# Preparing a scan layer's first chunk between the matmuls of the convolution before it

## The chip, the cores and the metric

The kernel runs on one core of one Trainium2 chip. All of it is float32. The metric is the device time of one execution in microseconds (us); of several runs the median is taken. The profile is of one execution. Engines are called PE (TensorE), DVE (VectorE), ACT (ScalarE), POOL (GpSimd) and SP (SyncE, which issues most of the DMAs); SBUF is the on-chip memory and PSUM the eight banks that matmuls write.

## The reference

Four residual layers on an image batch `x` of shape (3, 256, 48, 48). `_gn` is a group norm.

```python
x = x + _L0_conv_ref(_gn(x), ...)   # convolutions and attention blocks
x = x + _L1_conv_ref(_gn(x), L1_conv_routing_ws, L1_conv_weight)  # 3x3, weights mixed per image from 8 experts
x = x + _L2_conv_ref(_gn(x), L2_conv_weight, L2_conv_bias)        # 3x3
x = x + _L3_conv_ref(_gn(x), ...)   # selective scan (Mamba)
```

The change touches the border between the third and the fourth. The fourth takes the 2304 pixels of an image as a sequence `xf`:

```python
xn = (xf - mu) * jax.lax.rsqrt(var + 1e-05) * norm_w + norm_b     # over the 256 channels
x_in, z = jnp.split(jnp.einsum('blc,dc->bld', xn, in_proj_w), 2, axis=-1)
u = jax.nn.silu(depthwise causal conv of x_in over 4 positions + conv_b)
x_dbl = jnp.einsum('bld,ed->ble', u, x_proj_w)                    # dt_raw, B_ssm, C_ssm
dt = jax.nn.softplus(jnp.einsum('blr,dr->bld', dt_raw, dt_proj_w) + dt_proj_b)
# step: h = h * exp(dt_t * A) + dt_t * B_t * u_t;  y_t = h . C_t
y = (y + u * D_param) * jax.nn.silu(z)
out = jnp.einsum('bld,cd->blc', y, out_proj_w)
```

## The kernel before

**Layers 1 and 2** are one loop (L970 to L1002) over six units, layer by image, images in the order 2, 1, 0. Each unit has two halves `h`, each half two channel blocks `m`. An `output` (L943) makes six `products`: each is six matmul calls over 288 columns into one PSUM bank of the pool `ps` (seven banks, tag `c`). A call becomes two PE instructions. Products come as two pairs, each pair read by ACT (`cb`, L952) and DVE (`add`, `sub`, L954 and L956), then eight DVE updates of the image in SBUF (L961 to L964), then two single products, each read by one DVE update (L966). Beside them DVE transforms the next half's input (`input_transform`) and, in units 0 to 2, mixes the next unit's weights `u` (L271, L273). At the end of an image of layer 2 its six chunks are stored to DRAM (`xd`, L994) and its group norm is taken (matmuls L182 and L191, result in `norm3`).

**Layer 3** works in 18 chunks of 384 positions (six per image) and, per chunk, eight steps of eight scans (`scan`, L1378), so 144 steps. Before the scans a chunk is prepared by stages that the table `plan` lists, one after the other by their data: `fetch` (from `xd`), `group_scale` (ACT), `less_mean` (PE), `centre` (ACT), `square_mean` (PE), `inverse_root` (ACT), `normalise` (DVE), `tokens` (ACT), `taps` of four blocks (PE, with the weights `wtap`) and `take_u` (ACT), `silu` (ACT), `project_u` (PE), `take_dbc` (ACT, then DMAs to DRAM and back, spread over partitions: `bcd`, `bc`), and twice `project_dt` (PE), `softplus` (ACT), `take_dt` (DVE), `keep_dt` (ACT, then two DMAs `dtd`, `dtud`). All matmuls of these stages write the two banks of `psg`. `spread` (L1310) then brings rows of `dtd` and `dtud` back by eight DMAs, `fill` writes the scans' input (half on DVE, L1341, half on POOL, L1345), `decay` (ACT, L1370) the scans' factors, `times_c` (POOL, L1386) and `add_states` (PE, L1403) collect the result.

In the steady state the stages of the next two chunks are dealt out over the steps of the current one (`run`). For chunk 0 they stand in front of the first step, one after the other, and so do the first seven of chunk 1. Ahead of them come the layer's own weights: four DMAs for `cwb`, one each for `w3sb`, `dtsb` and `winx`, and four DVE products that make `wtap` (L1031).

**Memory.** The pools of layers 1 and 2 (weights `up0` and `up1`, images `x0` to `x2`, `vp`, `pad`, `wst`) are closed before layer 3 opens its own over the same addresses; a tile there waits until the old tile's last reader is done.

**Order.** In the scan (and in the attention of layer 0) `keep_order` ties the instructions of PE, DVE, ACT and POOL to the order in which the program writes them. Elsewhere, and for SP always, the framework puts each engine's instructions in order when the kernel is built: earlier in the program first, but past one that it reckons not ready. On the chip each engine then follows its list.

Of the kernel before, what the change touches and what calls it, by code (L numbers as in the profile page):

```python
# [16 lines left out]
P = 128  # L17
# [66 lines left out]
def net(  # L84
# [27 lines left out]
    late_pools = ExitStack()  # L112

    def late_pool(name, bufs=1):
        return late_pools.enter_context(tc.tile_pool(name=name, bufs=bufs, side="right"))
# [238 lines left out]
    with ExitStack() as l0:  # L354
# [482 lines left out]
        xs[2] = late_pool("x2").tile([P, CT, N], F32, name="x2")  # L837
        upools = {0: late_pool("up0")}
        for b in (1, 0):
            xs[b] = late_pool(f"x{b}").tile([P, CT, N], F32, name=f"x{b}")  # L840
# [51 lines left out]
        for n, b in enumerate(ORDER):  # L892
# [11 lines left out]
            for c in range(NCH):  # L904
                concatenated(b, c, *ahead.pop(0))
                z = n * NCH + c + 3
                if z < len(chunks):
                    ahead.append(parts(*chunks[z]))
                if c:
                    take_stats(b, c - 1, stats)  # L910
                if b == 0 and c == 3:
                    vp = late_pool("vp", 2)
                    pad = late_pool("pad")
                    first_v = input_transform(2, 0, *norms[2])
                aside(3)
# [10 lines left out]

    with ExitStack() as l1:
        upools[1] = l1.enter_context(tc.tile_pool(name="up1", bufs=1))
        tmp = l1.enter_context(tc.tile_pool(name="tmp", bufs=2))
        ps = l1.enter_context(tc.tile_pool(name="ps1", bufs=7, space=PSUM))  # L930
# [13 lines left out]
        def output(b, h, m, u, vt, bias):  # L944
# [4 lines left out]
            for i, j in ((1, 3), (4, 5)):  # L949
# [7 lines left out]
                sums += [add, sub]  # L957
            p, q, r, s = sums
# [6 lines left out]
            for i, k, f in ((0, 0, 1.5), (2, 3, 6.0)):  # L965
                stt(xj[:, k], products(u, vt, m, i), f, xj[:, k], ALU.mult, ALU.add)  # L966

# [12 lines left out]

        vt = first_v
        for n, (k, h) in enumerate(halves):
            layer, b = units[k]
            ahead = transformed(n + 1) if n + 1 < len(halves) else None
# [6 lines left out]
            if layer and h == 1:  # L991
# [10 lines left out]
                norm3[b] = keep[:, 0, :], keep[:, 1, :]  # L1002

    late_pools.close()
# [5 lines left out]
    with ExitStack() as l3:  # L1010
        wp = l3.enter_context(tc.tile_pool(name="w3", bufs=1))
        act = l3.enter_context(tc.tile_pool(name="act", bufs=2))
        psd = l3.enter_context(tc.tile_pool(name="psd", bufs=1, space=PSUM))
        psr = l3.enter_context(tc.tile_pool(name="psr", bufs=1, space=PSUM))
        psg = l3.enter_context(tc.tile_pool(name="psg", bufs=1, space=PSUM))
        psy = l3.enter_context(tc.tile_pool(name="psy", bufs=1, space=PSUM))

        w3sb = wp.tile([P, NW3], F32, name="w3sb")
        nc.sync.dma_start(w3sb, w3)
        dtsb = wp.tile([DTR + 1, DI * P], F32, name="dtsb")  # L1020
        nc.sync.dma_start(dtsb, dtw)

        wtap = wp.tile([P, DCONV, CT, DI * P], F32, name="wtap")
        with tc.tile_pool(name="w3in", bufs=1) as wi:
            winx = wi.tile([P, CT, DI * P], F32, name="winx")
            nc.sync.dma_start(winx, w3x.rearrange("(t p) n -> p t n", p=P))
            cwb = wi.tile([P, DCONV, DI * P], F32, name="cwb")
            for k in range(DCONV):
                nc.sync.dma_start(cwb[:, k, :], convw[k : k + 1, :].broadcast_to([P, DI * P]))
            for k in range(DCONV):  # L1030
                nc.vector.tensor_tensor(  # L1031
                    wtap[:, k, :, :], winx,
                    cwb[:, k, :].unsqueeze(1).broadcast_to([P, CT, DI * P]), ALU.mult,
                )

        scn = l3.enter_context(tc.tile_pool(name="scn", bufs=2))

        def w(name, at, n):
            a = W3_AT[name] + at
            return w3sb[:, a : a + n]  # L1040


        amat = wp.tile([P, DI * DS], F32, name="amat")
        nc.scalar.activation(amat, v("A_log", 0, DI * DS), AF.Exp)
        nc.vector.tensor_scalar(amat, amat, -1.0, None, ALU.mult)

        rep = wp.tile([P, 4, 32], F32, name="rep")
        for r in range(4):
            nc.vector.tensor_reduce(
                rep[:, r, :], ident.rearrange("p (q d) -> p d q", d=32), AX.X, ALU.add  # L1050
            )
        fold = rep[:, 0, :]

        less = wp.tile([P, 2, P], F32, name="less")
        nc.vector.tensor_tensor(less[:, 0, :], ident, mean2, ALU.subtract)
        nc.vector.tensor_scalar(less[:, 1, :], mean2, -1.0, None, ALU.mult)
        zero = wp.tile([P, 8], F32, name="zero")
        nc.vector.memset(zero, 0.0)
# [4 lines left out]

        todo = [(b, c) for b in ORDER for c in range(NCH)]

        def fetch(at):
            k = chunks[at] = Chunk()
            k.b, k.c = todo[at]
            k.before = chunks.get(at - 1)
            k.xp = act.tile([P, CT, CH], F32, name="xp", bufs=1)  # L1070
            nc.sync.dma_start(k.xp, xd[k.b][:, k.c])

        class Chunk:
            pass


        bank = [psg.tile([P, 512], F32, name=f"ps_g{j}")[:, :CH] for j in range(2)]

        def in_order(t):

            return t.rearrange("p (j n) -> p n j", j=4)

        def group_scale(k):
            sc, sh = norm3[k.b]
            k.xg = act.tile([P, CT, CH], F32, name="xg", bufs=1)
            for ct in range(CT):
                nc.scalar.activation(
                    k.xg[:, ct, :].rearrange("p (n j) -> p j n", j=4),  # L1090
                    k.xp[:, ct, :].rearrange("p (j n) -> p j n", j=4), AF.Identity,
                    bias=sh[:, ct : ct + 1], scale=sc[:, ct : ct + 1],
                )

        def less_mean(k):

            for to in range(CT):
                for ct in range(CT):
                    nc.tensor.matmul(  # L1099
                        bank[to], less[:, int(to != ct), :], k.xg[:, ct, :],  # L1100
                        start=ct == 0, stop=ct == CT - 1,
                    )

        def square_mean(k):
            for ct in range(CT):
                nc.tensor.matmul(
                    bank[1], mean2, k.sq[:, ct, :], start=ct == 0, stop=ct == CT - 1
                )

        def centre(k):  # L1110
            for ct in range(CT):
                nc.scalar.copy(k.xg[:, ct, :], bank[ct])
            k.sq = act.tile([P, CT, CH], F32, name="sq", bufs=1)
            nc.scalar.activation(k.sq, k.xg, AF.Square)

        def inverse_root(k):
            var = bank[1]
            nc.scalar.activation(var, var, AF.Ln, bias=epst)
            nc.scalar.activation(var, var, AF.Exp, scale=-0.5)

        def normalise(k):
            rs = bank[1].unsqueeze(1).broadcast_to([P, CT, CH])
            nc.vector.tensor_tensor(k.xg, k.xg, rs, ALU.mult)

        def tokens(k):

            xn = k.xn = act.tile([P, CT, CH + DCONV - 1], F32, name="xn")
            if k.c == 0:
                nc.gpsimd.memset(xn[:, :, : DCONV - 1], 0.0)
            else:  # L1130
                nc.scalar.copy(xn[:, :, : DCONV - 1], k.before.xn[:, :, CH:])
# [73 lines left out]
        def keep_dt(k, m0):  # L1205
            for j in range(2):
                nc.scalar.copy(k.dt[:, m0 + j, :], bank[j])  # L1207
            if m0 == 0:
                k.dtd, k.dtud = {}, {}
# [376 lines left out]
```

## Time and profile before

| | |
|---|---|
| median of 3 runs | 3690.63 us (3689.73 to 3693.51) |
| profiled execution | 3692.94 us, span 3691.2 us, granted PE clock 0.926 |
| PE busy | 3195.5 us, 87% of the span |
| DVE busy | 3058.3 us, 83% |
| ACT busy | 2265.2 us, 61% |
| POOL busy | 1440.4 us, 39% |

The span runs from the first to the last instruction, and times below count from its start; the execution's own time is 1.74 us more. The page cuts the span into 40 slices of 92 us and gives each engine's busy share in tenths. In other rows a name such as `ps_c<-vt,u` gives what is written and what is read, `x264` how many instructions are merged in the row, and a bracket the time that the engine stood idle before it and what it waited for. `PEclk` is the granted share of PE's clock. A row that begins with `SPq` is a DMA being issued, not its transfer.

### The profile page before, as it was taken

The numbers are of one execution on the slowest core, as the hardware profiler recorded it, in microseconds if no ns is written. First come the engines' busy times: TensorE is split into PE (matmuls) and PEld (weight loads), VectorE is DVE, ScalarE is ACT, GpSimd is POOL, SyncE is SP. The second block draws the span as 40 slices with busy tenths as digits, with TensorE's granted clock in tenths as the row PEclk, the third lists the DMA queues.
The fourth block names the chain that finished last, engine by engine and source line by source line (L and its number), as shares of the span: only waits on it lengthen the run. The fifth ranks groups of instructions, "written<-read, shape, count | busy, mean of one in ns | idle before, by whom it ended". The sixth has DMA issues, their size and how long they took to land. (4 is left out here: it accounts for less than half of the span.)

```text
span 3691.2 us, 45621 instructions
## 1 busy us (share of the span) xinstructions
PE 3195.5 (87%) x17154; PEld 1442.3 (39%) x17154; DVE 3058.3 (83%) x3398; ACT 2265.2 (61%) x3402; POOL 1440.4 (39%) x386
## 2 busy tenths in 40 slices
PE   6999999999999998777799857888878888888885
PEld 4323232342323224455577633333333333333331
DVE  3798999869889993589977429999999999999997
ACT  2688787758878773320011037777777777777774
POOL 0000000000000001110000009999999999999998
PEclk9999999999999999888899978999889999988887
DMA  4000000000000003645401234444444444444441
GB/s 176 4 1 1 1 2 1 1 39 1 2 1 2 1 1 112 211 149 197 165 13 26 67 85 95 99 106 112 108 110 109 105 105 99 106 115 106 112 106 35
DMA packets 167672, 266.50 MB, mean 72 GB/s; under 512 B 42689, under 2 KB 133633, under 8 KB 165266
## 3 DMA queue, kind: packets, MB, share of 16 engines
q1 hardware_dynamic: 155346, 245.80, 24.7%
q10 hardware_dynamic: 12096, 17.70, 1.5%
q8 instruction: 136, 2.23, 0.3%
q14 instruction: 94, 0.77, 0.1%
HBM read 216.31 MB, written 46.89 MB: 71 GB/s over the span
## 5 line engine op out<-in xcount | busy, mean ns | idle before, releaser
L597 ACT ACTIVATE pt<-ps_s 128x1024 f32<-128x1024 f32 x972 | 938.9, 1022 | 236.9 <-PE ps_s L593 219.1
L1378 DVE TENSOR_TENSOR_SCAN hs<-ps_da,hs 128x385 f32<-128x385 f32 x1152 | 1012.9, 940 | 60.2 <-ACT ps_da L1370 43.7
L673 DVE TENSOR_TENSOR part<-part,pt 128x2048 f32<-128x2048 f32 x396 | 906.5, 2289 | 79.4 <-ACT pt L597 54.8
L1386 POOL TENSOR_TENSOR hc<-hs,bc 128x3072 f32<-128x3072 f32 x144 | 888.2, 6169 | 85.8 <-PE ps_g L1186 28.6
L1370 ACT ACTIVATE ps_da<-dtr,amat 128x384 f32<-128x384 f32 x1152 | 657.8, 582 | 317.2 <-DVE hs L1378 289.2
L162 POOL TENSOR_TENSOR rstd<-ve,mhalf 128x2 f32<-128x2 f32 (+1 forms) x26 | 17.3, 668 | 1650.4 <-DVE ve L160 1650.4
L593 PE MATMUL ps_s<-q,kt 32*128 32x512 f32 (+1 forms) x4320 | 614.6, 592 | 2.3 <-DVE q L554 0.9
L1345 POOL TENSOR_TENSOR hs<-dtur,bc 128x1536 f32<-128x1536 f32 x144 | 496.4, 3447 | 95.9 <-DMA dtur<-dtud 85.2
L606 PE MATMUL acc<-pt,vt 128*32 128x512 f32 (+1 forms) x4320 | 521.3, 561 | 8.1 <-DVE o L653 7.9
L937 PE MATMUL ps_c<-vt,u 128*128 128x288 f32 x1728 | 429.4, 411 | 66.6 <-DVE u L259 39.4
L937 PEld LDWEIGHTS ps_c<-vt,u 128*128 128x128 f32 x1728 | 331.1, 192 | 159.3 <-issue 46.1
L1142 PE MATMUL ps_g<-xn,wtap 128*128 128x384 f32 x1152 | 387.1, 491 | 3.0 <-ACT xn L1133 3.0
L593 PEld LDWEIGHTS ps_s<-q,kt 32*128 32x128 f32 x4320 | 220.1, 183 | 387.6 <-issue 225.4
L1142 PEld LDWEIGHTS ps_g<-xn,wtap 128*128 128x128 f32 x1152 | 214.3, 189 | 174.7 <-issue 16.3
L1403 PE MATMUL ps_y<-hc,rep 128*32 128x384 f32 x2304 | 246.0, 550 | 28.4 <-POOL hc L1386 25.1
L1341 DVE TENSOR_TENSOR hs<-ps_r,bc 128x1536 f32<-128x1536 f32 x144 | 249.5, 1732 | 0.0
L606 PEld LDWEIGHTS acc<-pt,vt 128*32 128x32 f32 x4320 | 95.6, 108 | 363.1 <-issue 327.4
L952 ACT COPY cb<-ps_c 128x288 f32<-128x288 f32 x48 | 19.0, 397 | 342.5 <-PE ps_c L937 287.9
L1099 PE MATMUL ps_g<-xg,less 128*128 128x384 f32 x144 | 90.6, 805 | 98.7 <-ACT dt L1207 65.6
L1186 PE MATMUL ps_g<-dbc,dtsb 17*128 17x384 f32 x144 | 80.6, 694 | 102.0 <-ACT dt L1207 101.3
L1403 PEld LDWEIGHTS ps_y<-hc,rep 128*32 128x32 f32 x2304 | 64.5, 117 | 199.2 <-issue 149.5
L1217 PE MATMUL ps_g<-xn,w3sb 128*128 128x384 f32 x288 | 108.7, 510 | 28.6 <-ACT sz L1225 24.5
(211 smaller groups left out, 3170.8 us busy)
## 6 DMA issues: line engine op xcount, KB each, us to landing
wconv<-in_we SPq DMA_DIRECT2D x144, 384.0 KB, 4.4
dtr<-dtd SPq DMA_DIRECT2D x288, 192.0 KB, 3.8
bc<-bcd SPq DMA_DIRECT2D x144, 192.0 KB, 5.7
dtur<-dtud SPq DMA_DIRECT2D x288, 96.0 KB, 3.2
dtd<-dt SPq DMA_DIRECT2D x36, 384.0 KB, 2.4
yc<-ycat ACTq DMA_DIRECT2D x18, 576.0 KB, 5.5
xb<-in_x SPq DMA_DIRECT2D x6, 1152.0 KB, 11.0
ycat<-cur SPq DMA_DIRECT2D x6, 1152.0 KB, 4.2
```

The source lines that it names most:

```text
L593: nc.tensor.matmul(s[:, j, cols], kt[r, mt * P : (mt + 1) * P], q[r, :n], start=True, stop=True,)
L597: nc.scalar.activation(p[:, h0 : h0 + 2, :], s, AF.Exp)
L606: nc.tensor.matmul(acc[h * HD : (h + 1) * HD, :n], vt[:, mt, g * P + h * HD : g * P + (h + 1) * HD], p[:, h, cols], start=mt == 0, stop=mt ...
L673: nc.vector.tensor_tensor(part, first_p if group == 1 else part, p, ALU.add)
L937: nc.tensor.matmul(pc[:, :HN], u[:, i, dy, ct, m * P : (m + 1) * P], vt[:, i, ct, dy * TW : dy * TW + HN], start=ct == 0 and dy == 0, stop ...
L1142: nc.tensor.matmul(bank[m % 2], wtap[:, tap, ct, m * P : (m + 1) * P], k.xn[:, ct, tap : tap + CH], start=tap == 0 and ct == 0, stop=tap = ...
L1341: nc.vector.tensor_tensor(hs[:, :, 0:2, 1:], k.ps[:, :, :CH].unsqueeze(1).broadcast_to([P, 2, 2, CH]), bb, ALU.mult,)
L1345: nc.gpsimd.tensor_tensor(hs[:, :, 2:4, 1:], k.rows[m][1].unsqueeze(1).broadcast_to([P, 2, 2, CH]), bb, ALU.mult,)
L1370: nc.scalar.activation(slots[n % 3][:, 1 : CH + 1], chunks[at].rows[m][0][:, q, :], AF.Exp, scale=amat[:, col : col + 1],)
L1378: nc.vector.tensor_tensor_scan(b, slots[(8 * s + part) % 3][:, : CH + 1], b, 0.0, ALU.mult, ALU.add)
L1386: nc.gpsimd.tensor_tensor(hc, tiles[s][:, :, :, 1:], cb.broadcast_to([P, 2, 4, CH]), ALU.mult)
L1403: nc.tensor.matmul(k.y_ps[32 * q : 32 * q + 32, :CH], fold, hc[:, g, q, :], start=False, stop=h == 1 and g == 1,)
```

## The change

The stages of chunk 0 and the first seven of chunk 1 are written into the loop of layers 1 and 2. A generator, `early_preparation`, yields between pieces of them; `output` calls `between()` four times (after each pair of products and after each single one), and in units 4 and 5 each call runs the next piece. A half has two outputs, so a unit has 16 calls. What is left after the loop is run at once.

The memory is taken from tiles that are free by then: from unit 3 on the weights `up0` and the pieces `wst`, then image 2 after its store, then image 1 after its. One tile is cut into views (`divide`); chunk buffers are picked from `rooms` by chunk number, in the same depths as before (one or two), the second ones of `u`, `dtu`, `bc0`, `bc1` and `sz` being new tiles in layer 3. Weights of layer 3 are loaded at the start of unit 3 (`w3_loads`) and with the first piece (`winx`, `cwb`). The two banks of `psg` are open during layers 1 and 2, and `ps` has five banks in place of seven. Stage functions, `plan`, `after`, `gating` and the steps of the scan are moved in the file and otherwise as before.

```diff
-        ps = l1.enter_context(tc.tile_pool(name="ps1", bufs=7, space=PSUM))
+        ps = l1.enter_context(tc.tile_pool(name="ps1", bufs=5, space=PSUM))
...
+    psg = ctx.enter_context(tc.tile_pool(name="psg", bufs=1, space=PSUM))
+    rooms, w3v, chunks = {}, {}, {}
+    def room(k, name):
+        return rooms[name][k.at % len(rooms[name])]
+    def w3_rooms():
+        block = upools[0].tile([P, 6, 3, CT, 256], F32, name="u")
...
+            block, ("w3sb", P, (NW3,)), ("wtap", P, (DCONV, CT, DI * P)), ("dtsb", DTR + 1, (DI * P,)),
+            ("amat", P, (DI * DS,)), ("rep", P, (4, 32)), ("less", P, (2, P)), ("zero", P, (8,)),
+            ("xn0", P, (CT, CH + DCONV - 1)), ("xn1", P, (CT, CH + DCONV - 1)),
...
+    def x2_rooms():
+        block = xpools[2].tile([P, CT, N], F32, name="x2").rearrange("p a b -> p (a b)")
...
+        nc.sync.dma_start(winx, w3x.rearrange("(t p) n -> p t n", p=P))
+        for k in range(DCONV):
+            nc.sync.dma_start(cwb[:, k, :], convw[k : k + 1, :].broadcast_to([P, DI * P]))
+        for name, t in divide(
+            block, ("u", P, (DI, CH)), ("dtu", P, (DI, CH)), ("dt", P, (DI, CH))
...
+    def early_preparation():
+        exp_ln_tables()
+        fetch(0)
+        winx, cwb = x2_rooms()
+        k = chunks[0]
+        yield
+        group_scale(k)
+        yield
+        for tap in (0, 1):
+            fold_taps(winx, cwb, tap)
+        less_mean(k)
+        yield
+        centre(k)
+        yield
+        square_mean(k)
+        yield
+        for tap in (2, 3):
+            fold_taps(winx, cwb, tap)
+        inverse_root(k)
+        yield
+        normalise(k)
+        tokens(k)
+        fetch(1)
+        yield
+        for m in (0, 1):
+            taps(k, m, 0, 4)
+            yield
+        take_u(k, 0)
+        take_u(k, 1)
+        yield
+        for m in (2, 3):
+            taps(k, m, 0, 4)
+            yield
+        take_u(k, 2)
+        take_u(k, 3)
+        silu(k.u)
+        yield
+        while 1 not in norm3:
+            yield
+        x1_rooms()
+        yield
+        project_u(k)
+        yield
+        take_dbc(k)
+        yield
+        for m in (0, 2):
+            project_dt(k, m)
+            yield
+            softplus(k, m)
+            yield
+            take_dt(k, m)
+            yield
+            keep_dt(k, m)
+            yield
+        k = chunks[1]
+        for stage in (group_scale, less_mean, centre, square_mean, inverse_root, normalise):
+            stage(k)
+            yield
+        tokens(k)
...
                 sums += [add, sub]
+                between()
...
                 stt(xj[:, k], products(u, vt, m, i), f, xj[:, k], ALU.mult, ALU.add)
+                between()
...
+        early = early_preparation()
+        at_unit = 0
+        def between():
+            if at_unit >= 4:
+                next(early, None)
...
+            at_unit = k
+            if k == 3 and h == 0:
+                w3_rooms()
+                w3_loads()
...
+        for _ in early:
+            pass
...
-        for k in range(DCONV):
-            nc.vector.tensor_tensor(
-                wtap[:, k, :, :], winx,
...
         mark = listed[-1]
-        exp_ln_tables()
         last = len(todo) - 1
-        fetch(0)
-        fetch(1)
         k = chunks[0]
-        for _, _, _, stage in plan:
-            stage(k)
         k.rows = {0: spread(k, 0)}
...
-        for _, _, rel, stage in plan:
-            if rel == 2:
-                stage(chunks[1])
         for _, _, _, stage in gating:
             stage(k)
```

## The prediction

> **What bounds the kernel now.** I read the slices first, then engine times by stage, then the timeline across the border of two stages. The slices show two regimes: up to slice 23 TensorE (PE) is the full row, and from slice 25 VectorE (DVE) and GpSimd (POOL) are, with a dent between.
>
> ```profile
> PE   6999999999999998777799857888878888888885
> DVE  3798999869889993589977429999999999999997
> PEclk9999999999999999888899978999889999988887
> ```
>
> The stretches cut at the borders say what the dent is.
>
> ```profile
> core 0: us, PE busy (x) PEld busy (x) DVE busy (x) ACT busy (x) POOL busy (x), PEclk, DMA share, GB/s
> 1625.00:1819.00 194.00, 145.13 (x585) 112.51 (x585) 190.74 (x300) 18.20 (x26) 3.62 (x13) 0.87 0.56 193
> 1819.00:2105.00 286.00, 284.55 (x1172) 222.35 (x1172) 204.76 (x454) 29.89 (x45) 8.61 (x23) 0.99 0.10 25
> 2105.00:2127.00 22.00, 1.29 (x6) 0.97 (x6) 9.12 (x31) 2.85 (x4) 0.80 (x2) 0.56 0.81 237
> 2127.00:2182.00 55.00, 37.70 (x96) 19.61 (x96) 6.62 (x10) 19.03 (x29) 0.00 (x0) 0.81 0.21 48
> 2182.00:2202.00 20.00, 7.51 (x16) 3.78 (x16) 0.78 (x2) 6.36 (x11) 6.83 (x2) 0.64 0.83 188
> 2300.00:3691.00 1391.00, 1128.20 (x4641) 504.90 (x4640) 1271.36 (x1422) 1018.35 (x1935) 1287.18 (x272) 0.88 0.42 102
> ```
>
> From 1625 to 1819 (units 0 and 1 of the convolutions) DVE sets the pace: 190.74 of 194 us, mostly mixing weights. From 1819 to 2105 PE does: 284.55 of 286. From 2202 DVE does. Between them lie 97 us in which nothing is full: weights come in, then chunk 0 goes through a serial chain, then its rows are fetched back. Its ends, from the timeline:
>
> ```profile
> 2040.89 64.27 PE L937 MATMUL ps_c<-vt,u 128*128 128x288 f32 x264
> 2070.79 2.34 SPq L994 DMA_DIRECT2D xd<-x  x3
> 2105.19 0.46 DVE L966 SCALAR_TENSOR_TENSOR x<-ps_c,x 128x288 f32<-128x288 f32 x1 [0.38 <-PE ps_c L937]
> ...
> 2138.02 22.58 PE L1142 MATMUL ps_g<-xn,wtap 128*128 128x384 f32 x64 [2.97 <-ACT xn L1133]
> ...
> 2141.67 18.31 PEld L1142 LDWEIGHTS ps_g<-xn,wtap 128*128 128x128 f32 x57 [0.30 <-issue]
> ...
> 2182.19 0.54 SPq L1310 DMA_DIRECT2D dtr<-dtd  x1
> ...
> 2190.03 1.59 ACT L1370 ACTIVATE ps_da<-dtr,amat 128x384 f32<-128x384 f32 x3 [8.77 <-DMA dtr<-dtd]
> ...
> 2202.40 2.65 DVE L1378 TENSOR_TENSOR_SCAN hs<-ps_da,hs 128x385 f32<-128x385 f32 x3
> ```
>
> The last product ends at 2105.15 and the first scan starts at 2202.40: the gap is **97.25 us**. It is what the change works on.
>
> **Part 1: PE work moved ahead of the gap.** Units 4 and 5 have no free PE time, so each moved matmul pushes the last product back by its own length. One fp32 matmul call gives two instructions. Chunk 0: mean 4 calls, square 2, taps 32, `project_u` 4, `project_dt` 4, so 46; chunk 1: mean 4, square 2. That is 52 calls, 104 instructions. A warm one of 384 columns takes 18.31/57 = 0.321 us by the tap row (the products agree: 64.27/264 = 0.243 us for 288 columns, times 384/288 is 0.325). 104 x 0.321 = **33.4 us**.
>
> **Part 2: other work moved.** DVE: four `wtap` products (4.63 us in all), two `normalise` (0.95 each), four `take_dt` pairs (about 1.1 each), constants (about 2): some 13 us beside units 3 to 5, where DVE is busy 205 of 286 us. ACT: the stages of both chunks, at most 25.4 us (19.03 and 6.36 in the gap's rows), beside an ACT busy 30 of 286. Cost nothing while these covers hold; without them they would be waits of PE, which part 4 prices. DMA: `w3sb`, `dtsb`, `winx`, four `cwb`, two `xp`, ten of `bcd`/`bc`, four of `dtd`/`dtud`, all on SP, where in units 3 to 5 only the `xd` stores stand; the share there is 0.10. A load that waits for x2's memory holds up only `fetch(1)` and the next `xd` stores, which nothing needs before unit 5. POOL gets a memset of 0.11 us. Three table loads of 1.28 us lie on ACT.
>
> **Part 3: product banks 7 to 5.** The trace does not show five banks, so I laid it over the seven: I set the start of each of the 144 products against the end of the instruction that last reads the product five before it. In units 0 and 1 four products would start late, by up to 8.7 and 3.1 us; both units are followed by PE idling for the next weights, 27.19 and 21.57 us, which swallows it. In units 3 to 5 two would start late by 0.65 us, and the delays carried along come to 0.8.
>
> ```profile
> 1725.84 71.52 PE L937 MATMUL ps_c<-vt,u 128*128 128x288 f32 x288 [27.19 <-issue]
> 1818.92 41.24 PE L937 MATMUL ps_c<-vt,u 128*128 128x288 f32 x158 [21.57 <-DVE u L259]
> 1861.61 0.35 PE L182 MATMUL ps_gm<-mv,gmat 128*128 128x2 f32 x2 [1.45 <-DVE mv L179]
> ```
>
> A rule speaks against this: the Trainium skill, "Perfetto Trace Analysis", section "Optimization Strategy", says that the same gap repeating on the engine that should be full can mean too little PSUM for the next tile. By that rule each of the 16 outputs of units 2 to 5 could show a bubble; at the 0.65 of the overlay that is 10 us. The overlay finds two, so I take **0.8**, from 0 to 10.
>
> **Part 4: waits of PE in between (S).** A matmul dealt in before its operand is ready holds up all products behind it. The Trainium skill, "TensorE: Matmul & The Clock Gate", section "Step-by-step: what each phase is for", says that matmuls stay in program order and only weight loads are pulled ahead. By that rule alone the chain would keep its idle: from the first matmul of the chain (2126.83) to the last of `keep_dt` (2181.16) are 54.3 us with 29.6 of PE work, and chunk 1 takes 12.3 (2191.56 to 2203.83) with 3.9. So S is at most 24.7 + 8.4 = 33. The nearest row is the group norm's matmuls, dealt between products in the same way: six norms with two steps each, and PE waited 1.45 and a few tenths in all. The slots speak for the small end: a product takes 12 x 0.243 = 2.9 us, so slots are 5.8, 5.8, 2.9, 2.9 us apart, and between two dependent matmul stages lie two or more slots nearly everywhere. The tightest is `square_mean` to the taps: 11.6 us for `inverse_root` 1.1, two folds 2.3, `normalise` 1, `tokens` 1.3, and a DVE that may stand in 4 us of updates. I take **S = 3.5**, nearest the norm row with eleven stages in place of twelve and longer inputs, from 0 to 33.
>
> **Part 5: what is left of the gap.** After the last product come its update (0.5), three `xd` stores ahead of the rows on SP (2.34, as in the 2070.79 row), eight row loads and their landing (2182.19 to 2190.03: 7.84), one decay (0.6) and 0.2 of signalling: **11.5 us**. Diagonals, banks, state copies, DVE's half of `fill` (1.75) and chunk 1's `normalise` lie inside. Low end 9 (rows before stores). High end 19: the memory of a stored image came free 10.4 us after the last update before (the token memset at 2116.11 waited for `xd`), and 7.84 and 0.6 would follow that. POOL's half of `fill` (3.4) starts with the rows; the scans that need it are the fifth on, about 4 us after the first. Gating matmuls and copies kept their place before, and keep it: from first scan to end stays 3691.2 - 2202.4 = 1488.8 us.
>
> **The sum**, against the profiled execution (3692.94; 1.74 lies around its span): 33.4 + 0.8 + 3.5 + 11.5 = 49.2 take the place of 97.25, a gain of 48.1, so 3644.9. That execution is 2.3 above the median 3690.63; against the median it is 3642.6, said **3643**.
>
> **Rivals.** First (B), *PE waits in the slots*: the order on PE is fixed at build time from estimates, and any chip stage slower than its estimate (a table load, a DMA landing under `group_scale`) stops the products. Against it speak the slots and the norm row; for it, that this chain is longer than any dealt in so far. Waits of 10 to 33, or a hand-over of 19 in place of 11.5, give 3650 to 3680, middle 3660.
>
> Second (C), *the other side*: in the scan the buffers are now views of shared blocks, and a write that is made to wait for readers of a neighbouring view would stall in each of 144 steps (10.3 us each). 48.1/144 = 0.33 us a step eats the gain; 0.39 makes it slower by 0.2%. DVE's idle before scans is 60.2 us in all, 0.42 a step, so such a wait would nearly double it. Against it: the depths (one or two) are what they were, and the four engines' order there is still written out. If it happens, 3700 or more.
>
> Third (D), *more than forecast*: the rows land sooner, or SP's new order in the scan trims DVE's waits for `ps_da` (43.7 us): 3625 to 3634.
>
> Fourth (E), *it doesn't do what it says*: the chain, last in every engine's order, ends up behind the products after all. Then only the loads go, at most from 2105.15 to 2126.83, 21.7 us: 3669; with the 10 us of bubbles from part 3 and a stage or two of the chain waiting for memory, 3680 to 3690.
>
> **How the numbers follow.** The forecast A (S under 12, hand-over under 15; 3634 to 3655) gets 0.66, B 0.20, C 0.05, D 0.06, E 0.03. A measurement tells about 0.2%, 7 us. A, B, D and a third of E are faster: 0.93; the rest of E and a fifth of C the same: 0.03; the rest of C slower: 0.04. The range 3631 to 3664 holds A, somewhat over half of B and a third of D, about 0.8.
>
> **What would show it.** PE nearly full to a last product at about 2143 on the old scale, with 104 instructions of 384 columns in units 4 and 5 at 0.32 us; PE's waits for ACT or DVE before them under 6 us in sum; first scan 10 to 15 us after the last product; 1489 us from there to the end; PE idle still after units 0 and 1. A PE idle of over 10 us inside units 4 and 5 or bubbles on `ps_c` mean B; a longer stretch after the first scan means C. The forecast is wrong if the weights of units 1 or 2 come later than before, because DVE's order changed with five banks: every us there moves the end by one.

## The result, and the profile after

| | before | after |
|---|---|---|
| median, us | 3692.07 (3689.73 to 3693.51, 4 runs) | 3650.98 (3647.35 to 3654.68, 4 runs) |
| profiled execution, us | 3692.94, span 3691.2 | 3652.18, span 3650.2 |
| last product ends, us from the span's start | 2105.15 | 2139.24 |
| first scan starts, us after that | 97.25 | 16.28 |
| first scan to the end, us | 1488.80 | 1494.67 |

The ratio is 0.9889, with a 95% interval of 0.9872 to 0.9906: faster by 41.1 us, where 3643 was forecast, a gain of 48. The profiled execution ended at 3652.18 in place of 3644.9.

The slices of the changed kernel, in tenths of busy time:

```profile
PE   6999999999999998877799987878888888878885
PEclk9999999999999999888899988988888999988887
```

PE is now full in slices 21 to 23 and the dent behind them is shallower. The stretches of the changed kernel, cut at its own borders (columns as in the header):

```profile
core 0: us, PE busy (x) PEld busy (x) DVE busy (x) ACT busy (x) POOL busy (x), PEclk, DMA share, GB/s
1819.00:2139.00 320.00, 318.83 (x1276) 241.33 (x1276) 216.17 (x476) 62.30 (x89) 8.72 (x24) 0.99 0.17 47
2260.00:3650.00 1390.00, 1125.53 (x4628) 504.30 (x4624) 1269.90 (x1420) 1017.13 (x1931) 1285.86 (x271) 0.87 0.41 102
```

Units 2 to 5 hold 1276 matmul instructions in place of 1172: the 104 of the forecast. PE idles 1.2 of 320 us there, while ACT went from 29.9 to 62.3 beside it. PE in this stretch, from the timeline (dealt-in pieces stand between products), and its row in the chain of waits:

```profile
1978.67 2.74 PE L1053 MATMUL ps_g<-wconv,u 128*128 128x384 f32 x8
...
1989.98 1.45 PE L1060 MATMUL ps_g<-wconv,mean 128*128 128x384 f32 x4
...
2002.91 5.33 PE L1095 MATMUL ps_g<-u 128*128 128x384 f32 x16
```

```profile
engine line waited for: us in total, times, longest us
PE ps_c L1331 <- DVE u L259: 21.8, 1, 21.8
PE ps_gm L182 <- DVE mv L179: 1.2, 1, 1.2
```

No bracket stands in the PE rows: `less_mean` (1978.67), `square_mean` (1989.98) and the first taps (2002.91) are executed among the products without a wait, and what ACT and DVE do between them lies under product rows. The only long wait, 21.8, is that for unit 2's weights, which the kernel before has too (21.57).

The hand-over, from the timeline of the changed kernel:

```profile
2136.17 3.07 PE L1331 MATMUL ps_c<-vt,u 128*128 128x288 f32 x12
2139.62 0.45 DVE L1361 SCALAR_TENSOR_TENSOR x<-ps_c,x 128x288 f32<-128x288 f32 x1
2140.09 2.83 SPq L1401 DMA_DIRECT2D xd<-x  x3
2147.53 1.76 DVE L1474 TENSOR_TENSOR hs<-ps_r,x 128x1536 f32<-128x1536 f32 x1 [2.99 <-DMA xd<-x]
2147.62 0.32 SPq L1444 DMA_DIRECT2D dtr<-dtd  x1
2154.90 1.59 ACT L1503 ACTIVATE ps_da<-dtr,u 128x384 f32<-128x384 f32 x3 [7.02 <-DMA dtr<-dtd]
2155.52 2.66 DVE L1511 TENSOR_TENSOR_SCAN hs<-ps_da,hs 128x385 f32<-128x385 f32 x3 [6.24 <-ACT ps_da L1503]
2156.96 2.93 PE L1172 MATMUL ps_g<-u 128*128 128x384 f32 x4 [13.86 <-ACT x L1180]
...
2160.45 5.49 PE L1172 MATMUL ps_g<-u 128*128 128x384 f32 x8 [0.57 <-ACT x L1180]
2166.97 2.66 DVE L1511 TENSOR_TENSOR_SCAN hs<-ps_da,hs 128x385 f32<-128x385 f32 x3 [4.25 <-ACT ps_da L1503]
```

Two things in it were not in the sum. SP issues the first row load at 2147.62, 4.7 us after it has issued the stores, and DVE's fill at 2147.53 waits for the same stores (`DMA xd<-x`). And after the first scan come the matmuls of gating: the four products of chunk 0's gate `z` on PE (L1172), copied from PSUM by ACT (L1180). Their matmuls of 384 columns take 5.49/8 = 0.69 us each, twice the 0.32 of a warm one, behind 13.86 us of idle PE; the sixth scan starts only at 2166.97.

The gap against the forecast is 3650.2 - (3644.9 - 1.74) = 7.0 us of span. It splits at two marks: to the last product 2139.24 against 2142.85 (-3.6), from there to the first scan 16.28 against 11.5 (+4.8), from there to the end 1494.67 against 1488.8 (+5.9).

### The profile page after: what moved, and what is told of

Its sections match the earlier page's. It is cut to its first block, busy times and chain, and to the rows that moved or that the text cites. A ratio compares the mean times of both kernels' runs of the same rounds, so it can differ in the third digit from the quotient of the medians.

```text
span 3650.2 us, 45624 instructions
## 1 busy us (share of the span) xinstructions
PE 3195.5 (88%) x17154; PEld 1440.2 (39%) x17154; DVE 3058.1 (84%) x3398; ACT 2272.8 (62%) x3408; POOL 1440.6 (39%) x386
## 5 line engine op out<-in xcount | busy, mean ns | idle before, releaser
L1503 ACT ACTIVATE ps_da<-dtr,u 128x384 f32<-128x384 f32 x1152 | 657.8, 582 | 314.6 <-DVE hs L1511 289.0
L1519 POOL TENSOR_TENSOR hc<-hs,x 128x3072 f32<-128x3072 f32 x72 | 444.4, 6172 | 48.6 <-PE ps_g L1141 15.6
L1519 POOL TENSOR_TENSOR hc<-hs,bc 128x3072 f32<-128x3072 f32 x72 | 444.0, 6167 | 36.2 <-PE ps_g L1141 13.6
L1095 PE MATMUL ps_g<-u 128*128 128x384 f32 x1152 | 385.9, 490 | 0.0
L1095 PEld LDWEIGHTS ps_g<-u 128*128 128x128 f32 x1152 | 213.9, 189 | 170.2 <-issue 11.2
L1536 PE MATMUL ps_y<-hc,u 128*32 128x384 f32 x2304 | 244.1, 547 | 27.2 <-POOL hc L1519 23.9
L1478 POOL TENSOR_TENSOR hs<-dtur,x 128x1536 f32<-128x1536 f32 x72 | 247.8, 3442 | 19.4 <-DMA dtr<-dtd 11.5
L1478 POOL TENSOR_TENSOR hs<-dtur,bc 128x1536 f32<-128x1536 f32 x72 | 248.2, 3447 | 8.1 <-ACT ps_g L1073 4.9
L1141 PE MATMUL ps_g<-wconv,u 17*128 17x384 f32 x144 | 79.2, 684 | 97.2 <-ACT x L1162 97.2
L1172 PE MATMUL ps_g<-u 128*128 128x384 f32 x288 | 112.7, 526 | 39.1 <-ACT x L1180 23.3
L1053 PE MATMUL ps_g<-wconv,u 128*128 128x384 f32 x144 | 87.9, 784 | 67.3 <-ACT x L1162 67.3
```

The lines of the kernel that those rows point to most:

```text
L1095: nc.tensor.matmul(bank[m % 2], w3v["wtap"][:, tap, ct, m * P : (m + 1) * P], k.xn[:, ct, tap : tap + CH], start=tap == 0 and ct == 0, sto ...
L1172: nc.tensor.matmul(bank[j], w("in", ct * 512 + m * P, P), k.xn[:, ct, DCONV - 1 :], start=ct == 0, stop=ct == CT - 1,)
L1478: nc.gpsimd.tensor_tensor(hs[:, :, 2:4, 1:], k.rows[m][1].unsqueeze(1).broadcast_to([P, 2, 2, CH]), bb, ALU.mult,)
L1503: nc.scalar.activation(slots[n % 3][:, 1 : CH + 1], chunks[at].rows[m][0][:, q, :], AF.Exp, scale=amat[:, col : col + 1],)
L1519: nc.gpsimd.tensor_tensor(hc, tiles[s][:, :, :, 1:], cb.broadcast_to([P, 2, 4, CH]), ALU.mult)
L1536: nc.tensor.matmul(k.y_ps[32 * q : 32 * q + 32, :CH], fold, hc[:, g, q, :], start=False, stop=h == 1 and g == 1,)
```

## Experiments

The theories after the comparison of the two traces. **M**: the rows wait because the scan's pool lies in part over image 0, and every tile in it waits until image 0 is stored. **W**: PE's clock is low after the idle, and the gating stages hold up the decays behind them. **G**: gating, in its old place, is itself late in the order now that the gap is short. Rivals: the row loads or SP's queue set the hand-over whatever the pool; the scan's shared views slow each step (C of the prediction); five banks cost or save something; the gain comes from early loads alone (E).

The marks of each profiled execution, and the times. Scan 8 is the one of index 8, the first of the scan's second step.

| | last product | first scan after it | scan 8 after first scan | first scan to end | median, us | ratio to before, 95% |
|---|---|---|---|---|---|---|
| before | 2105.15 | 97.25 | 12.26 | 1488.80 | | |
| after | 2139.24 | 16.28 | 15.86 | 1494.67 | 3650.98 | 0.9889 (0.9872 to 0.9906) |
| own pool for `hc` | 2136.06 | 13.46 | 15.72 | 1494.05 | 3647.07 | 0.9876 (0.9860 to 0.9893) |
| gating first | 2141.80 | 16.73 | 8.78 | 1486.06 | 3642.71 | 0.9860 (0.9843 to 0.9876) |
| PE kept warm | 2139.23 | 16.71 | 11.86 | 1489.52 | 3645.46 | 0.9871 (0.9855 to 0.9888) |
| before, five banks | 2100.71 | 98.62 | 13.63 | 1488.99 | 3693.08 | 1.0001 (0.9992 to 1.0010) |
| nothing dealt out | 2107.34 | 73.52 | 13.23 | 1489.25 | 3671.68 | 0.9936 (0.9921 to 0.9951) |
| taps twice | 2147.02 | 14.84 | 15.54 | 1493.66 | 3656.88 | 0.9900 (0.9882 to 0.9917) |
| chunk 1 late | 2135.53 | 29.34 | 16.17 | 1494.81 | 3660.01 | 0.9904 (0.9889 to 0.9920) |
| gap filled | 2136.35 | 14.41 | 8.66 | 1485.42 | 3638.37 | 0.9845 (0.9832 to 0.9859) |
| rows before stores | 2133.93 | 14.41 | 8.66 | 1486.49 | 3636.38 | 0.9841 (0.9828 to 0.9855) |
| `dtr` rows first | 2135.47 | 14.41 | 8.66 | 1485.66 | 3635.03 | 0.9842 (0.9829 to 0.9856) |

The first product starts anywhere from 1622.3 to 1628.0 in these executions, and units 0 and 1 vary by a few us more; the last product's column carries that. Where a few us matter below, the stretch is taken from the group norm's matmuls in unit 4 (the first L182 row there). Of the versions of the changed kernel, the intervals of own pool, gating first, PE kept warm, taps twice and chunk 1 late overlap that of the changed kernel itself; there the marks inside one execution carry the argument, not the medians.

**Own pool for `hc`.** In the memory map of the changed kernel, image 0 lies under the double-buffered tile `hc` alone, but `hc` is in one pool with the row tiles and the scan's inputs. The edit puts `hc` in a pool of its own; all addresses stay.

```diff
         scn = l3.enter_context(tc.tile_pool(name="scn", bufs=2))
+        hcp = l3.enter_context(tc.tile_pool(name="hcp", bufs=2))
...
-            hc = scn.tile([P, 2, 4, CH], F32, name="hc")
+            hc = hcp.tile([P, 2, 4, CH], F32, name="hc")
```

> Edit: in the changed kernel the tiles hc get a pool of their own; every address stays what it was, and only hc's still lies over image 0 and its stores. Theory M (a tile of a pool waits until everything under the whole pool's addresses is free, so the row loads waited for the stores of image 0 to land): row loads start about 3.5 us after the last product instead of 8.4, first scan about 11.5 to 12.5 us after it instead of 16.3, end about 4 us earlier than the changed kernel (3650.98 to about 3647). Rival Q (the loads stand behind the stores in SP's queue or on the DMA engines): hand-over stays within 1 us of 16.3, time within 1.5 us of the changed kernel.

SP's queue and the first decay in the timeline of this kernel, whose last product ends at 2136.06:

```profile
2136.18 0.32 SPq L1445 DMA_DIRECT2D dtr<-dtd  x1
2136.91 3.94 SPq L1401 DMA_DIRECT2D xd<-x  x3
2140.89 1.17 SPq L1445 DMA_DIRECT2D dtur<-dtud  x1
...
2148.90 1.59 ACT L1504 ACTIVATE ps_da<-dtr,u 128x384 f32<-128x384 f32 x3 [10.95 <-DMA dtr<-dtd]
```

The first row load is issued 0.12 us after the last product in place of 8.38. M is confirmed: the wait was for the whole pool's memory. But the first scan comes 13.46 us after the last product where 11.5 to 12.5 were expected; the gain is 2.8 us. One load goes out, and then the three stores take SP for 3.94 us ahead of the other rows. The wait became a place in a queue, which is the rival's part.

**Gating first.** The four gating stages are written ahead of the state copy, the fill and the first decays, instead of behind them.

```diff
         spread_pe(k, 0)
+        for _, _, _, stage in gating:
+            stage(k)
         first_states(0)
         fill(0)
         for n in range(3):
             decay(n)
-        for _, _, _, stage in gating:
-            stage(k)
```

> Edit: in the changed kernel the gating stages of chunk 0 are written ahead of the first state copy and the first three decays instead of behind them. Theory G (the scans of step 0 were held by ACT, which stood in the gating copies between decays 2 and 3 while PE did the gating products at its low clock): scans 3 to 7 follow one another without the holes, scan 8 comes about 7 to 9 us after the first scan instead of 15.9, and the time falls by 6 to 8 us (3650.98 to about 3644). Rival H (the holes come from POOL's half of the fill or from rows landing late): scan 8 stays within 1.5 us of where it was relative to the first scan.

The gating matmuls in the timeline of this kernel:

```profile
2146.11 1.56 PE L1172 MATMUL ps_g<-u 128*128 128x384 f32 x4 [0.45 <-ACT x L1180]
...
2148.23 2.85 PE L1172 MATMUL ps_g<-u 128*128 128x384 f32 x8 [0.57 <-ACT x L1180]
```

They run while the rows are still on their way, and warm. The first decay is not earlier (16.73 to the first scan), but scan 8 comes 7.1 us sooner and the end 8.6 us sooner. So what stands between the first decays and the later ones is gating, as G and W both said; this run alone can't tell the order from the clock.

**PE kept warm.** The order stays, and the first gating product is issued ten times more, with the same values into the same bank, to fill PE's idle time.

```diff
         spread_pe(k, 0)
+        for _ in range(10):
+            project_z(k, 0, 0)
         first_states(0)
```

> Edit: in the changed kernel ten more copies of the first gating product (40 instructions, same result in the same bank) stand before it, where PE is idle between the last product and the gating. Nothing else moves; extra work is done, nothing is left out. Theory W (3.6 us of step 0 were lost because PE had been idle 14 us and its granted clock had fallen, so that the gating products took 0.64 us an instruction and not 0.32): the second to fourth gating products take about half as long, scan 5 comes 8 to 9 us after the first scan instead of 11.45, time down by 2 to 3.5 us. Rival O (order alone, not the clock): scan 5 stays at 11 to 11.5 us after the first, time unchanged within 1 us.

A stretch of 14 us from the first scan on, of the changed kernel first and then of this one (columns as above: the one to read is PEclk, third from the end):

```profile
2156.00:2170.00 14.00, 12.48 (x25) 6.58 (x26) 7.01 (x9) 6.34 (x14) 6.62 (x3) 0.65 0.33 76
```

```profile
2156.00:2170.00 14.00, 12.15 (x38) 6.89 (x38) 10.92 (x12) 10.31 (x18) 10.64 (x3) 1.00 0.37 82
```

And the gating matmuls in this kernel's timeline, to lay beside the 2.93 and 5.49 of the changed kernel:

```profile
2157.38 1.56 PE L1172 MATMUL ps_g<-u 128*128 128x384 f32 x4 [1.28 <-ACT x L1180]
...
2159.50 2.85 PE L1172 MATMUL ps_g<-u 128*128 128x384 f32 x8 [0.57 <-ACT x L1180]
```

With the granted clock at 1.00 instead of 0.65, the same instructions in the same order take half, and scan 8 comes 4.0 us sooner. That is the clock's part, and it is more than was expected: the median is 5.5 us lower and not 2 to 3.5, scan 5 follows the first after 7.45 us and not after 8 to 9. From first scan to end it is 5.2; the 1.2 that come behind scan 8 are not traced, and the three kernels with a filled gap below, alike in that part, differ by 1.1 there (1476.76, 1477.83 and 1477.00 from scan 8 to the end). The Trainium skill, "TensorE: Matmul & The Clock Gate", section "What's actually happening", says that PE falls to half its clock after an idle window of about 3.4 us; here 13.86 us of idle and then twice the time for an instruction agree with it (0.65 is the mean over a stretch that ends warm: 0.50 up to 2165.70, 0.98 from there). The other 3.1 us by scan 8 that gating first brings (8.78 against 11.86) are the order, and the kernel before pays them too: its scan 8 comes after 12.26.

**Before, with five banks.**

```diff
-        ps = l1.enter_context(tc.tile_pool(name="ps1", bufs=7, space=PSUM))
+        ps = l1.enter_context(tc.tile_pool(name="ps1", bufs=5, space=PSUM))
```

> Edit: the kernel before with five product banks instead of seven, nothing else. Forecast of part 3: last product 0 to 0.8 us later, PE idle after units 0 and 1 shorter by up to 9 and 3 us, time within 1 us of the kernel before. Rival (bubbles by the rule on too little PSUM): PE waits between products in units 2 to 5, last product up to 10 us later. Since the changed kernel's last product came only 34.1 us later with 33.4 of added matmuls, I expect 0 to 0.5.

First to last product: 478.07 us against 480.04 before, and a ratio of 1.0001 (0.9992 to 1.0010). Five banks cost nothing.

**Nothing dealt out.** The pieces stay in the generator, with all early loads and memory, but are run after the loop.

```diff
-            if at_unit >= 4:
+            if at_unit >= 6:
```

> Edit: in the changed kernel nothing is dealt out; the whole preparation is written behind the loop of layers 1 and 2, in the same rooms, with the weights loaded in unit 3 as in the changed kernel. If the gain comes from chunk 0's chain running beside products: the last product comes 30 to 34 us earlier than in the changed kernel, but the chain runs serially after it, and first scan comes 70 to 78 us after the last product (97.25 before, less the 21.7 us of loads); end 20 to 28 us later than the changed kernel, about 3675. Rival (the planner deals the stages out by itself where it finds room, the written places don't matter): within 6 us of the changed kernel.

The taps in the timeline of this kernel, whose last product ends at 2107.34; ahead of them the L182 mark of unit 4, of the kernel before, of the changed kernel and of this one:

```profile
1967.34 0.28 PE L182 MATMUL ps_gm<-mv,gmat 128*128 128x2 f32 x2
```

```profile
1967.07 0.28 PE L182 MATMUL ps_gm<-mv,gmat 128*128 128x2 f32 x2
```

```profile
1969.52 0.28 PE L182 MATMUL ps_gm<-mv,gmat 128*128 128x2 f32 x2
...
2117.40 22.57 PE L1095 MATMUL ps_g<-u 128*128 128x384 f32 x64 [4.25 <-ACT u L1087]
```

From the L182 mark to the last product it takes 137.82 us, the kernel before 137.81; the taps stand in one row again, behind the products. The chain starts at once (its weights and input are there), yet the first scan comes 73.5 us after the last product. Early memory and loads are worth 97.3 - 73.5 = 23.7 us of hand-over, or 22.3 in the medians (3671.68 against 3694.01 for the kernel before, run beside it). By the spans they are worth 3691.2 - 3670.1 = 21.1, and dealing brings the other 3670.1 - 3650.2 = 19.9. In this kernel each makes about half of the gain, and E, which leaves only the first, is not what happened. The first half is a low figure: this chain waits for five ACT table loads of 1.28 us (one in `inverse_root`, two in each `softplus`) that the kernel before does not have there, up to 6.4 us; where they come from is told in the last section.

**Taps twice.** Half of the tap matmuls are issued twice into the same bank: 32 more instructions in slots of unit 4.

```diff
         for m in (0, 1):
             taps(k, m, 0, 4)
+            taps(k, m, 0, 4)
             yield
```

> Edit: in the changed kernel the tap products of blocks 0 and 1 of chunk 0 are done twice in their slots, 32 more instructions of 384 columns with the same result. If PE is full in units 4 and 5 and a dealt-in matmul costs its own length (part 1): last product 32 x 0.321 = 10.3 us later, time up by 10 to 10.5 us, to about 3661. Rival (products have slack, dealt-in matmuls partly fill holes): time up by 0 to 5 us.

From the L182 mark to the last product it takes 182.49 us, against 172.17 in the changed kernel: 10.32, or 0.3225 for each of 32. So PE has no slack at all in unit 4, and each dealt-in matmul moves the last product by its length. The medians differ by 5.9 us, not 10.3, but this kernel's times spread over 14.5 us (3650.21 to 3664.68), and its profiled execution began with units 0 to 3 1.5 us shorter and had a hand-over 1.4 us shorter.

**Chunk 1 late.** Chunk 1's seven stages go back behind the first decays, where the kernel before has them.

```diff
-        k = chunks[1]
-        for stage in (group_scale, less_mean, centre, square_mean, inverse_root, normalise):
-            stage(k)
-            yield
-        tokens(k)
...
         for n in range(3):
             decay(n)
+        for _, _, rel, stage in plan:
+            if rel == 2:
+                stage(chunks[1])
```

> Edit: in the changed kernel the first seven stages of chunk 1 go back to where they stood before, behind the first three decays and ahead of the gating; chunk 0 stays dealt out. By the sum: 12 instructions, 3.9 us, less ahead of the last product; the first scan waits for chunk 1's normalise as it did before, 11.8 us after the first decay; PE is then warm for the gating, 3.6 us back. Together 3 to 8 us slower than the changed kernel, first scan 27 to 31 us after the last product. Rival (the wait for the rows hides the chunk's stages, and dealing them out cost 3.9 us for nothing): 2 to 5 us faster.

The last product is 3.7 us earlier, of which 12 x 0.32 = 3.9 was to come; the first scan is 13.1 us later after it. The timeline of this kernel:

```profile
2150.50 1.59 ACT L1498 ACTIVATE ps_da<-dtr,u 128x384 f32<-128x384 f32 x3
...
2153.14 5.39 PE L1053 MATMUL ps_g<-wconv,u 128*128 128x384 f32 x8 [14.38 <-ACT wconv L1043]
...
2159.99 1.28 ACT L1072 ACT_TABLE_LOAD   x1
...
2162.20 1.28 ACT L1073 ACT_TABLE_LOAD   x1
...
2166.71 2.93 PE L1172 MATMUL ps_g<-u 128*128 128x384 f32 x4 [3.83 <-ACT x L1180]
...
2170.20 5.39 PE L1172 MATMUL ps_g<-u 128*128 128x384 f32 x8 [0.57 <-ACT x L1180]
```

The same gating matmuls in the kernel before, behind the same chain:

```profile
2204.24 1.56 PE L1217 MATMUL ps_g<-xn,w3sb 128*128 128x384 f32 x4 [2.55 <-ACT sz L1225]
...
2206.36 2.85 PE L1217 MATMUL ps_g<-xn,w3sb 128*128 128x384 f32 x8 [0.57 <-ACT sz L1225]
```

The decays are done by 2152.1, but the first scan starts at 2164.87: DVE executes its list in order, and `normalise` (at 2164.00, behind this chain) stands ahead of the scan. The chain's first matmuls are at the low clock again, 5.39/8 = 0.67 us. In all it is 9.0 us slower in the medians, where 3 to 8 were expected. The 3.6 us that a warm gating was to bring back did not come: the chain has two table loads that the one of the kernel before has not, and the second, 1.28 us, stands on ACT ahead of gating's first copy. PE is idle for 3.83 us before the next gating product, in place of 2.55, and the granted clock behind it is 0.50 (2166.60 to 2175.40) in place of 1.00 (2204.00 to 2209.00). Scan 8 is at 16.17.

**Gap filled.** The own pool, and the PE stages of chunk 1 and gating alternating in the gap before the first decays, where PE is idle anyway; only `group_scale` of chunk 1 stays dealt in.

```diff
+        hcp = l3.enter_context(tc.tile_pool(name="hcp", bufs=2))
...
-        for stage in (group_scale, less_mean, centre, square_mean, inverse_root, normalise):
-            stage(k)
-            yield
-        tokens(k)
+        group_scale(k)
...
         fill(0)
+        one = chunks[1]
+        less_mean(one)
+        centre(one)
+        square_mean(one)
+        project_z(k, 0, 0)
+        inverse_root(one)
+        take_z(k, 0, 0)
+        project_z(k, 1, 0)
+        normalise(one)
+        take_z(k, 1, 0)
+        project_z(k, 2, 0)
+        tokens(one)
+        project_z(k, 3, 1)
...
-        for _, _, _, stage in gating:
-            stage(k)
```

> Edit: the changed kernel with hc in a pool of its own, and with chunk 1's PE stages and chunk 0's gating written ahead of the first decays, where every engine waits for the rows. If the three losses add up: last product 3.9 us earlier, hand-over about 13.5 us, step 0 without holes (scan 8 at 8.8 us): 13 to 15 us faster than the changed kernel, 3636 to 3638. Rival (the chain of chunk 1 with its table loads takes longer than the rows and holds the decays on ACT): first scan 16 to 19 us after the last product, 3640 to 3643.

It is 12.6 us faster than the changed kernel (13 to 15 were expected), with intervals that do not touch. The span's 14.0 us split into 2.9 (12 fewer instructions between products, less what varies ahead of them), 1.9 at the hand-over and 9.3 after the first scan. The hand-over is 14.41, though the rows are no longer late: something else ends last. Three changes stand in this kernel at once; their parts are told apart by these marks and the runs above, not one by one.

**Rows before stores, and `dtr` rows first.** Two ways to bring the rows sooner still, on top of the last kernel: the last three stores of image 0 behind the first rows (its pool closed after them), and then also the four `dtr` loads ahead of the four `dtur` loads.

```diff
+                store_chunks(0, NCH if b else 3)
...
         k.rows = {0: spread(k, 0)}
+        store_chunks(3, NCH)
+        x0_pools.close()
+        hcp = l3.enter_context(tc.tile_pool(name="hcp", bufs=2))
```

```diff
-            for i in range(4):
-                r = slice(32 * i, 32 * i + 32)
-                for t, src in ((dtr, k.dtd), (dtur, k.dtud)):
-                    src = src[m & 2][:, m & 1, :]
+            for t, src in ((dtr, k.dtd), (dtur, k.dtud)):
+                src = src[m & 2][:, m & 1, :]
+                for i in range(4):
+                    r = slice(32 * i, 32 * i + 32)
```

> Edit: the gap-filled kernel, with the last three stores of image 0 written behind chunk 0's first row loads instead of ahead of them (image 0's memory is given back after them). If the three stores, 2.83 us of SP's time and 1.15 MB on the DMA engines, are what still lies between the last product and the rows: first decay about 9 to 11 us after the last product instead of 13.8, first scan 10 to 12 us after it, 2.5 to 4 us faster than the gap-filled kernel (3638.4 to about 3635). Rival (the chain of chunk 1 on ACT, done 13.8 us after the last product there, is the bound): no change within 1 us.

> Edit: the kernel with rows before stores, and in each row fetch the four dtr loads ahead of the four dtur loads instead of alternating. If the first decay still waits for the fourth dtr load: it starts up to 1.4 us earlier and the time falls by 0 to 1.5 us. If ACT's chain of chunk 1 is the bound by now, or POOL's half of the fill, which gets its rows later: no change or up to 1 us slower.

The rows were to bring the first scan 10 to 12 us after the last product; the rival came true. In all three kernels the first decay starts 13.80 us and the first scan 14.41 us after the last product, to a hundredth. The timeline of the second of them, whose last product ends at 2133.93:

```profile
2141.97 6.81 POOL L1477 TENSOR_TENSOR hs<-dtur,x 128x1536 f32<-128x1536 f32 x2 [2.26 <-DMA dtur<-dtud]
...
2142.24 1.28 ACT L1073 ACT_TABLE_LOAD   x1
...
2146.53 1.31 ACT L1087 ACTIVATE u<-wconv,vec 128x384 f32<-128x384 f32 x2
...
2147.74 2.18 ACT L1502 ACTIVATE ps_da<-dtr,u 128x384 f32<-128x384 f32 x4
```

POOL's half of the fill has its rows at 2141.97; the decay starts 5.8 us later, directly behind `tokens` of chunk 1 on ACT. So with the gap filled it is ACT's list that sets the hand-over, a table load of 1.28 us among it, and sooner rows do not help. The three medians, 3635 to 3638, are not told apart. They are the fastest versions here. Writing the first decays ahead of chunk 1's last stages was not tried.

## Why the prediction was right, and where it was wrong

The direction, the mechanism and the range were right. The size was 7 us too good, and that is three terms, one of them the other way: 10.7 us were missing and 3.6 came back from waits that did not occur. That the sum came so near is in part luck.

**Parts 1, 3 and 4: to the last product, 37.7 forecast, 34.1 measured.** The count of 104 held. From the L182 mark, the last product came 172.17 - 137.81 = 34.4 us later, 0.330 us for each; doubling some of them gave 0.3225. The forecast 33.4 was right, and so was its reason. The 0.8 for the banks and the 3.5 for waits were not needed: the banks cost nothing in the run that isolates them, and PE's waits between products in units 2 to 5 are one wait for the group norm, 1.2 us in place of the 1.45 of before. Of the two rules that were weighed neither showed: no bubbles for want of banks, and none of the chain's idle in PE's row. That the slots were wide enough is the likely reason for the second; no run made them narrower. Rival B was wrong for units 4 and 5; what remains of it is that the hand-over was above 15, against A's own condition, though the time lies in A's range and just inside B's lower end.

**Part 2: other work hidden.** Held, though one count in it was low: three table loads of 1.28 us were said, and the stages in units 4 and 5 brought eight, 10.2 us (95 against 89 in the whole kernel). With 62 of 320 us busy beside the products ACT hid them all; that was a wide cover, not a forecast. In the filled gap, one such load stands in the chain that ends last.

**Part 5: 11.5 forecast, 16.28 measured. The step that failed first.** It put three stores (2.34) and the rows right behind them on SP. The rows waited for the stores to land, 4.7 us more, because the pool they are in overlaps image 0: the wait is not for the last reader of the old tile under a new one, as the description of the memory has it, but for all that lies under the pool. Part 5 wrote such a wait as its high end, 19, and put it at nothing in the middle without a reason. The other terms were near: 2.83 for the stores, 7.28 from the first row load to the decay. What the reserve of 19 assumed (10.4 us from update to free memory) was 7.5 here. The run with its own pool shows the cause; that the gain was then 2.8 and not 4.7 agrees with the stores being next in SP's queue, where the timeline shows them.

**"From first scan to end stays 1488.8": 1494.67. The step that failed second.** Gating keeps its place in the order, as the step said, but not its cost. In the kernel before, chunk 1's chain stands in the gap until 2203.83, and the gating matmuls behind it take 1.56 and 2.85 us. With chunk 1 dealt out, PE has nothing for 13.86 us, and gating finds it at half clock. Scan 8 is 3.6 us later after the first than before, and the warm-PE run returns 4.0 there; of the 5.9 us to the end it returns 5.2. So taking work out of a gap had a price that no row of the work itself shows: it had kept the clock up.

**Rival C** is refuted by the same marks, though its sign, a longer stretch after the first scan, was there: the sign did not tell a stall in every step from a loss at the start. Against the kernel before, scan 8 is 3.6 us later after the first scan, the first scan of the ninth step 5.4, that of the 73rd 6.1, and the end 5.9. So 3.6 us are lost in the first step and 1.9 in steps 5 to 8, and the 136 steps behind them are as before, within 0.7 in all. Where the 1.9 come from was not traced; the warm-PE run has 1.2 of them too, so the clock in the first step does not account for all. **Rival D** did not occur either: nothing in the steady scan gained. **Rival E**, had it come true, would look like the run with nothing dealt out: 3671.68, near the 3669 that was said for it.

## What to carry to other kernels

When work is pulled out of a gap, draw up what the gap looks like afterwards: which memory is freed last and by which pool, what is next in the queue that wait leaves, and how long TensorE then stands idle, since here the next matmuls paid for it. Work that fits into the idle time of the gap is better left there than paid for on a full engine: here the best version deals out the long chain and keeps some twelve matmuls and the gating in the gap. A new allocation over old memory waits at the granularity of the pool, so a tile that overlaps late memory belongs in a pool of its own. And an instruction that no data ties to its place, such as the request for a table set, may not move with the code around it: look in the trace where it was executed.

## What the runs showed of the hardware

After 13.86 us without work PE ran 384-column matmuls at 0.64 to 0.69 us, not 0.32. It kept that for some 9 us (2156.96 to 2165.73), through a burst of 2.93 us, a pause of 0.57 and a burst of 5.49; of the row that follows without a pause the first 13 take 4.44/13 = 0.34 each. A pause of 2.55 us ahead of gating left the granted clock at 1.00 (kernel before), one of 3.83 left it at 0.50 (chunk 1 late). In the warm-PE run, with 40 useless matmuls ahead of the scan, the time from first scan to end is 5.2 us shorter.

`Ln` and `Exp` share a table set, which the kernel asks for by `exp_ln_tables` (L225) ahead of the chain and again after `silu`. In the kernel before these requests are executed there, and no `Ln` or `Exp` of the chain behind them loads a table:

```profile
2105.46 1.28 ACT L225 ACT_TABLE_LOAD   x1
...
2164.02 1.28 ACT L225 ACT_TABLE_LOAD   x1
```

In the changed kernel the requests of chunk 0 are written outside the scan, where order is not tied. No L225 row stands in units 4 and 5; there is one at the very start, and the `Ln` and the `Exp` of `inverse_root` each load a table:

```profile
0.80 1.28 ACT L225 ACT_TABLE_LOAD   x1 [0.80 <-PEq L1699]
...
1990.60 1.28 ACT L1072 ACT_TABLE_LOAD   x1
...
1992.47 1.28 ACT L1073 ACT_TABLE_LOAD   x1
```

That the request went to the start because no data ties it is likely from the ordering rule, and not tested. In the fastest versions the load of 1.28 us ahead of the first decay (2142.24 above) is of this kind; a version that ties the request to its place was not run.
